# Spreading layer 0's dst values along the free axis: a DMA through DRAM in place of a 0/1 matmul

## The chip, the cores and the metric

The kernel runs on one core of one Trainium2 chip. The metric is the device time of one launch in microseconds (us). Three runs of the kernel before gave a median of 3661.84 us (3660.82 to 3661.86).

## The reference

The input is 128 graphs of 64 nodes with 768 features, all in fp32, and one 64 x 64 adjacency mask per graph. Two graph-attention layers follow each other; each is followed by a residual sum and a layernorm. The change touches layer 0 only:

```python
h = jnp.einsum('bnd,ade->bane', feat_in, W)              # 12 heads of 64
th = jnp.tanh(h)
attn_src = jnp.einsum('bane,aeo->bano', th, w_src)       # one value per node and head
attn_dst = jnp.einsum('bane,aeo->bano', th, w_dst)
attn = attn_src + jnp.swapaxes(attn_dst, 2, 3)           # score[n, m] = src[n] + dst[m]
attn = jnp.where(attn >= 0, attn, LEAKY_ALPHA * attn)
attn = jnp.where(~adj[:, None, :, :], -999.0, attn)
attn = jax.nn.softmax(attn, axis=-1)
feat_out = jnp.einsum('banm,bame->bane', attn, h) + b
# elu, then a gate: sigmoid(x @ H_w.T + H_b) mixes elu(feat_out) with x
```

Layer 1 is ordinary masked attention with 6 heads of 128 (q, k, v and an output product).

The point that matters: a score is a sum of one value of the query node n and one value of the key node m. With the query nodes on the partitions, `src[n]` is one value per partition, but `dst[m]` has to lie along the free axis and be the same on all partitions of the graph. The sums over features leave it the other way round, with node m on partition m.

## The kernel before

A *tile* is 128 tokens on the 128 partitions, which is two graphs of 64 nodes; there are 64 tiles. A *group* is two tiles (G = 2). Layer 0 works in *units*: half of the heads (6) of one tile, so there are 128 units, 4 in a group. Layer 1 works by groups.

All weights are loaded into SBUF once at the start, by DMAs issued from SyncE's queue (SP): first the first two tiles of x, then W, the broadcast vectors, H_w (transposed on TensorE), and the four weights of layer 1. The tiles of x have seven buffers, so they are loaded well ahead. Every load and store in the kernel is issued from SP.

One unit of layer 0 goes like this:

- `l0_products(u)`: the tile is transposed on TensorE (L170, first half only), and multiplied with `w_sb` (L177; 6 products of 128x384, each in two fp32 passes). VectorE (DVE) copies the result to `h` (L246), ScalarE (ACT) takes its tanh `th` (L248), GpSimd (POOL) multiplies with the src weights (L250), DVE sums over the features (L252), and POOL and DVE do the same for dst (L255, L256). Both sums are in `sd`. Then POOL builds `dg` (L261): six 64 x 64 diagonal matrices, one for each head, with dst on the diagonal. After that comes the gate's product with `hw_sb` (L177), its bias (L271) and its tanh (L272).
- `l0_probs(u)`: one matmul (L280) multiplies `same_graph`, a 0/1 matrix with a one wherever two partitions belong to the same graph, with `dg`. Its result `pd` in PSUM holds dst[m] on all partitions of the graph. DVE adds src (L282), takes the leaky part (L283); POOL and DVE apply the mask (L284, L287); `softmax` follows (L185 to L194: DVE, ACT, DVE, and POOL at the end).
- `l0_probs_transposed(u)`: TensorE transposes the probabilities (L202), and ACT and DVE copy them to `pts[0]` (L209).
- `l0_rest(u)`: the products of probabilities and `h` (L303), the elu, the gate and the residual (L308 to L324), and after a tile's second half the layernorm (L214 to L220).

The main loop goes through the units and does parts of a unit one step late, with pieces of layer 1 in between:

```python
    for u in range(NT * 2 + LAG):
        ...
            l0_products(u)
        if 0 < u <= NT * 2:
            l0_probs_transposed(u - 1)
        fill(quota // 3)
        if u < NT * 2:
            l0_probs(u)
        if 0 < u <= NT * 2:
            l0_rest(u - 1)
        fill(quota - quota // 3)
```

`fill(n)` takes pieces of layer 1 from a list until their weight reaches n: scores of one head (5; L345, L355, L358), values (4; L177 with `wv_sb`), context (2; L379, L388) and result (4; L177 with `wf_sb`, L396, then layernorm and the store at L399). The list of a group is filled at step u = 4q + 1 and lasts for four steps. The pieces of steps 0 to 5 are missing, since no group is through layer 0 yet.

The order on each engine is set by a scheduler when the program is built. It follows the source's order as a priority, but an instruction whose inputs it expects to be ready may be placed ahead of one that is earlier in the source. All waits between engines are inserted automatically, and each engine then runs its own list in order.

Of the kernel before, what the change touches and what calls it, by code (L numbers as in the profile page):

```python
# [9 lines left out]
F32 = mybir.dt.float32  # L10
U8 = mybir.dt.uint8
AF = mybir.ActivationFunctionType
ALU = mybir.AluOpType
AX = mybir.AxisListType

P = 128
# [7 lines left out]
def kernel(  # L24
# [17 lines left out]
    bf: bass.AP,  # L42
    out: bass.AP,
):
    """Two graph-attention layers, each followed by a residual and a layernorm.

    A tile is 128 tokens on the partitions: two graphs of 64 nodes. A group is G tiles, whose
    q and k share a pass over the weights. All products are in fp32.
    """
    nc = tc.nc  # L50
    NB, S, D = x.shape
    A, _, E = W.shape
# [3 lines left out]
    HALF = D // 2  # L56
    AH = A // 2
    CH = NC // 2
    G = 2
# [8 lines left out]
    const = ctx.enter_context(tc.tile_pool(name="const", bufs=1))  # L68
    xp = ctx.enter_context(tc.tile_pool(name="xp", bufs=7))
    big = ctx.enter_context(tc.tile_pool(name="big", bufs=1))  # L70
    work = ctx.enter_context(tc.tile_pool(name="work", bufs=2))
    small = ctx.enter_context(tc.tile_pool(name="small", bufs=3))
    psm = ctx.enter_context(tc.tile_pool(name="psm", bufs=4, space=bass.MemoryType.PSUM))
    psa = ctx.enter_context(tc.tile_pool(name="psa", bufs=4, space=bass.MemoryType.PSUM))

# [1 line left out]
    ident = const.tile([P, P], F32, name="ident")  # L77
    make_identity(nc, ident)
    eye = const.tile([P, S], F32, name="eye")
    nc.vector.tensor_add(eye, ident[:, :S], ident[:, S:])  # L80
    same_graph = const.tile([P, P], F32, name="same_graph")
    nc.vector.memset(same_graph, 0.0)
    for g in range(2):
        nc.vector.memset(same_graph[g * S : (g + 1) * S, g * S : (g + 1) * S], 1.0)
    neg_half = const.tile([P, 1], F32, name="neg_half")
    nc.vector.memset(neg_half, -0.5)

    xs, adjs = {}, {}
# [10 lines left out]
        load_x(t)  # L99
    load_adj(0)  # L100

# [1 line left out]
    def rows(src, name):  # L103
        n = src.shape[0]
        t = const.tile([P, n], F32, name=name)
# [15 lines left out]
    for oc in range(NC):  # L121
        hrow = xp.tile([P, D], F32, name="x")
        nc.sync.dma_start(hrow, H_w[oc * P : (oc + 1) * P, :])
        for half in range(2):
            ps = psa.tile([P, CH, P], F32, name="pa")
            for c in range(CH):
                k = half * CH + c
# [23 lines left out]
    bv_c = columns(bv, "bv_c")  # L151
    bf_bc = rows(bf, "bf_bc")

    # Transposed probabilities of AH heads, block-diagonal over the tile's two graphs: only the
    # diagonal blocks are written after this. One for each layer.
    pts = [const.tile([P, AH, P], F32, name=f"pt{i}") for i in range(2)]
    for pt in pts:
        nc.gpsimd.memset(pt, 0.0)

# [1 line left out]
    def halves(h):  # L161
        return slice(h * HALF, (h + 1) * HALF)

    def transposed(src, dst):
        """dst[:, c, :] = src[:, chunk c].T"""
        for half in range(2):
            ps = psa.tile([P, CH, P], F32, name="pa")
            for c in range(CH):
                k = half * CH + c
                nc.tensor.transpose(ps[:, c, :], src[:, k * P : (k + 1) * P], ident)  # L170
            nc.any.tensor_copy(dst[:, half * CH : (half + 1) * CH, :], ps)  # L171

    def product(lhsT, w, half):
        """One half of the columns of lhsT.T @ w in PSUM."""
        ps = psm.tile([P, HALF], F32, name="pm")
        for c in range(NC):
            nc.tensor.matmul(  # L177
                ps, lhsT[:, c, :], w[:, c, halves(half)], start=(c == 0), stop=(c == NC - 1)
            )
        return ps  # L180

    def softmax(s, n):
        """Over the last of s [P, n, S], in place."""
        mx = small.tile([P, AH], F32, name="mx")
        nc.vector.tensor_reduce(mx[:, :n], s, AX.X, ALU.max)  # L185
        nc.vector.tensor_tensor(
            s, s, mx[:, :n, None].to_broadcast([P, n, S]), ALU.subtract
        )
        nc.scalar.activation(s, s, AF.Exp)
        sm = small.tile([P, AH], F32, name="sm")  # L190
        nc.vector.tensor_reduce(sm[:, :n], s, AX.X, ALU.add)
        rs = small.tile([P, AH], F32, name="rs")
        nc.vector.reciprocal(rs[:, :n], sm[:, :n])  # L193
        nc.gpsimd.tensor_tensor(  # L194
            s, s, rs[:, :n, None].to_broadcast([P, n, S]), ALU.mult
        )

    def probs_transposed(s, pt):
        """s [P, AH, S] over (graph, query) -> [(graph, key), head, (graph, query)]."""
        ps = psa.tile([P, AH // 2, P], F32, name="pa")  # L200
        for j in range(AH // 2):
            nc.tensor.transpose(  # L202
                ps[:, j, :], s[:, 2 * j : 2 * j + 2, :].rearrange("p h m -> p (h m)"), ident
            )
        pt_v = pt.rearrange("p (j h) n -> p j h n", h=2)
        for g in range(2):
            own = slice(g * S, (g + 1) * S)
            for h2 in range(2):
                nc.any.tensor_copy(pt_v[own, :, h2, own], ps[h2 * S : (h2 + 1) * S, :, own])  # L209
# [20 lines left out]
        nc.vector.tensor_scalar(f1, a, 1.0, -L1_NEG, op0=ALU.subtract, op1=ALU.mult)  # L230
        masks[g] = (a, f0, f1)

# [1 line left out]
    xTs, units = {}, {}  # L234

    def l0_products(u):
        t, half = divmod(u, 2)
        hs = halves(half)
        if half == 0:
            xTs[t] = work.tile([P, NC, P], F32, name="xT")  # L240
            transposed(xs[t], xTs[t])
        xT = xTs[t] if half == 0 else xTs.pop(t)

        ph = product(xT, w_sb, half)
        h = work.tile([P, HALF], F32, name="h", bufs=3)
        nc.vector.tensor_copy(h, ph)  # L246
        th = work.tile([P, HALF], F32, name="th")
        nc.scalar.activation(th, ph, AF.Tanh)  # L248
        tmp = work.tile([P, HALF], F32, name="tmp", bufs=3)
        nc.gpsimd.tensor_tensor(tmp, th, ws_bc[:, hs], ALU.mult)  # L250
        sd = small.tile([P, 2, AH], F32, name="sd")
        nc.vector.tensor_reduce(  # L252
            sd[:, 0, :], tmp.rearrange("p (a e) -> p a e", a=AH), AX.X, ALU.add
        )
        nc.gpsimd.tensor_tensor(th, th, wd_bc[:, hs], ALU.mult)  # L255
        nc.vector.tensor_reduce(  # L256
            sd[:, 1, :], th.rearrange("p (a e) -> p a e", a=AH), AX.X, ALU.add
        )
        # dst on the diagonal: what same_graph spreads along the free axis
        dg = work.tile([P, AH, S], F32, name="tmp", bufs=3)  # L260
        nc.gpsimd.tensor_tensor(  # L261
            dg,
            eye[:, None, :].to_broadcast([P, AH, S]),
            sd[:, 1, :, None].to_broadcast([P, AH, S]),
            ALU.mult,
        )

        # gate = (1 + tanh(y / 2)) / 2
        pg = product(xT, hw_sb, half)
        gt = work.tile([P, HALF], F32, name="gt")  # L270
        nc.vector.tensor_tensor(gt, pg, hb_bc[:, hs], ALU.add)  # L271
        nc.scalar.activation(gt, gt, AF.Tanh, scale=0.5)  # L272
        units[u] = [h, gt, sd, dg]

    def l0_probs(u):
        g, i = divmod(u // 2, G)
        adjf, fill0, _ = masks[g]
        _, _, sd, dg = units[u]
        pd = psa.tile([P, AH, S], F32, name="pa")
        nc.tensor.matmul(pd, same_graph, dg, start=True, stop=True)  # L280
        s = work.tile([P, AH, S], F32, name="s0")
        nc.vector.tensor_tensor(s, pd, sd[:, 0, :, None].to_broadcast([P, AH, S]), ALU.add)  # L282
        nc.vector.scalar_tensor_tensor(s, s, LEAKY_ALPHA, s, op0=ALU.mult, op1=ALU.max)  # L283
        nc.gpsimd.tensor_tensor(  # L284
            s, s, adjf[:, i, None, :].to_broadcast([P, AH, S]), ALU.mult
        )
        nc.vector.tensor_tensor(  # L287
            s, s, fill0[:, i, None, :].to_broadcast([P, AH, S]), ALU.add
        )
        softmax(s, AH)  # L290
        units[u][2:] = [s]
# [4 lines left out]
    def l0_rest(u):  # L296
# [5 lines left out]
        for a in range(AH):  # L302
            nc.tensor.matmul(  # L303
                po[:, a, :], pts[0][:, a, :], h[:, a * E : (a + 1) * E], start=True, stop=True
            )
        # elu(z) + 1 = max(z, 0) + exp(min(z, 0))
        z = work.tile([P, HALF], F32, name="z")
        nc.vector.tensor_tensor(  # L308
            z.rearrange("p (a e) -> p a e", a=AH),
# [1 line left out]
            b_bc[:, None, :].to_broadcast([P, AH, E]),  # L311
            ALU.add,
        )
        e = work.tile([P, HALF], F32, name="tmp", bufs=3)
        nc.vector.tensor_scalar_min(e, z, 0.0)  # L315
        nc.scalar.activation(e, e, AF.Exp)  # L316
        nc.vector.scalar_tensor_tensor(z, z, 0.0, e, op0=ALU.max, op1=ALU.add)
        nc.vector.scalar_tensor_tensor(
            z, z, 1.0, xt[:, hs], op0=ALU.subtract, op1=ALU.subtract
        )  # L320
        # the residual's sum, doubled, as the layernorm's epsilon then is fourfold:
        # 2 * (2 * x + gate * (elu - x)) = 4 * x + (1 + tanh(y / 2)) * (elu - x)
        nc.vector.scalar_tensor_tensor(z, gt, 1.0, z, op0=ALU.add, op1=ALU.mult)  # L323
        nc.vector.scalar_tensor_tensor(  # L324
            xt[:, hs], xt[:, hs], 4.0, z, op0=ALU.mult, op1=ALU.add
# [1 line left out]
        if half == 1:  # L327
            layernorm(xt, 4.0 * EPS)

# [1 line left out]
    def layer1(g):  # L331
        x1T = big.tile([P, NC, G, P], F32, name="x1T")
        for i in range(G):
# [39 lines left out]
        def context(i):  # L373
            cTs[i] = work.tile([P, HEADS, P], F32, name="cT", bufs=1)
            for half in range(2):
                pc = psa.tile([P, CH, P], F32, name="pa")
                for j in range(CH):
# [5 lines left out]
                        start=True,  # L383
                        stop=True,
                    )
                # a row's probabilities sum to one, so v's bias goes straight to the context
                hds = slice(half * CH, (half + 1) * CH)
                nc.vector.tensor_tensor(  # L388
                    cTs[i][:, hds, :], pc, bv_c[:, hds, None].to_broadcast([P, CH, P]), ALU.add
# [25 lines left out]
        pieces += [(4, result, (G - 1, 0)), (4, result, (G - 1, 1))]  # L415
        return pieces

# [1 line left out]
    assert G == 2  # L419
    UG = 2 * G  # L420
    LAG = 2
# [62 lines left out]
```

## Time and profile before

| What | Value |
|---|---|
| median of three runs | 3661.84 us (3660.82 to 3661.86) |
| span of the profiled execution, first to last instruction | 3657.3 us |
| the runs above that span | 3.5 to 4.6 us |
| TensorE matmul (PE) busy | 3605.6 us, 99% |
| VectorE (DVE) / ScalarE (ACT) / GpSimd (POOL) busy | 47% / 22% / 23% |
| granted TensorE clock, mean | 0.997 |
| DMA of the hardware queue | 66.64 MB, 5.3% of 16 engines' span |

The profile is of one execution; of that execution it gives the span, and no time of its own beside it. The runs' time holds what lies around the span. A group of instructions shows its line, engine, operation, tiles (out<-in), shapes, count, then total busy time and the mean of one in ns, and after them the idle time of the engine just before these instructions with what ended it. PEld is TensorE's weight load, which lies beside its matmuls. Matmuls are pipelined, so the mean of one is longer than its share of TensorE; the distance from start to start is the better measure. SPq is SyncE's queue, which issues the DMAs. In the steady part a group of four units takes 112.6 us.

### The profile page before, as it was taken

Reading aid. Unit: us, or ns where it says so; the run is one execution under the profiler, and the core shown is the slowest. Engines: PE = TensorE matmul, PEld = TensorE weight load, DVE = VectorE, ACT = ScalarE, POOL = GpSimd, SP = SyncE. Lnnn points to the kernel's source line nnn. Section 1 sums busy time; section 2 is a strip of 40 time slices with the busy share of each in tenths; the row PEclk is TensorE's granted clock in tenths of the full one; section 3 lists DMA queues with packets and bytes.
Section 4 is the critical chain, followed back from the end, with each engine's and each line's share of the span. In section 5 each row is a group of like instructions: output and inputs, shape, how many; then the busy total and the mean of one; then the engine's idle time right before and its main releaser. Section 6 shows DMA issues by size and latency. Waiting matters only on the chain.

```text
span 3657.3 us, 40929 instructions
## 1 busy us (share of the span) xinstructions
PE 3605.6 (99%) x16228; PEld 2544.3 (70%) x16228; DVE 1721.5 (47%) x3821; ACT 810.4 (22%) x1925; POOL 852.3 (23%) x904
## 2 busy tenths in 40 slices
PE   6999999999999999999999999999999999999999
PEld 4776677766777666777667776677766677766776
DVE  4545444544444454444544454444445444454442
ACT  2222222222222222222222222222222222222221
POOL 2222212222222222122222222222222222222120
PEclk9999999999999999999999999999999999999999
DMA  6000000000000000000000000000000000000000
GB/s 204 1 18 18 18 10 9 18 18 18 9 10 18 18 18 10 9 18 18 18 18 9 9 18 18 18 9 10 18 18 18 9 10 18 18 18 14 5 5 18
DMA packets 44031, 69.25 MB, mean 19 GB/s; under 512 B 23104, under 2 KB 23104, under 8 KB 43840
## 3 DMA queue, kind: packets, MB, share of 16 engines
q1 hardware_dynamic: 43840, 66.64, 5.3%
q8 instruction: 128, 2.10, 0.2%
q14 instruction: 63, 0.52, 0.0%
HBM read 41.46 MB, written 25.17 MB: 18 GB/s over the span
## 4 chain that ended last, share of the span: by engine, by line
PE 88%; DVE 9%; POOL 1%; ACT 1%; SPq 0%; issue 0%; DMA 0%; POOLq 0%; ACTq 0%
PE pm L177 47%; PE pm L345 28%; PE pa L303 3%; PE pa L280 3%; PE pa L379 2%; PE pa L355 2%; PE pa L202 1%; DVE st L214 1%; POOL s L284 1%; DVE x L396 1%; PE pa L170 1%; DVE z L323 1%; DVE s L287 1%; DVE x L324 1%; DVE mx L185 1%; DVE s L283 1%
## 5 line engine op out<-in xcount | busy, mean ns | idle before, releaser
L345 PE MATMUL pm<-x1T,wq_sb 128*128 128x256 f32 x2304 | 560.3, 384 | 0.3 <-DVE x1T L171 0.3
L177 PE MATMUL pm<-w_sb,xT 128*128 128x384 f32 x1536 | 534.3, 494 | 13.9 <-DVE xT L171 13.4
L345 PE MATMUL pm<-x1T,wk_sb 128*128 128x256 f32 x2304 | 528.6, 379 | 0.0
L177 PE MATMUL pm<-wv_sb,x1T 128*128 128x384 f32 x1536 | 519.8, 488 | 0.0
L177 PE MATMUL pm<-wf_sb,cT 128*128 128x384 f32 x1536 | 517.9, 487 | 0.4 <-DVE cT L388 0.4
L177 PE MATMUL pm<-hw_sb,xT 128*128 128x384 f32 x1536 | 516.3, 486 | 0.0
L345 PEld LDWEIGHTS pm<-x1T,wk_sb 128*128 128x128 f32 x2304 | 437.8, 190 | 59.5
L345 PEld LDWEIGHTS pm<-x1T,wq_sb 128*128 128x128 f32 x2304 | 424.9, 190 | 62.6 <-DVE x1T L171 0.6
L177 PEld LDWEIGHTS pm<-hw_sb,xT 128*128 128x128 f32 x1536 | 291.8, 190 | 203.5
L177 PEld LDWEIGHTS pm<-w_sb,xT 128*128 128x128 f32 x1536 | 284.6, 190 | 199.8 <-DVE xT L171 21.1
L177 PEld LDWEIGHTS pm<-wf_sb,cT 128*128 128x128 f32 x1536 | 286.9, 190 | 187.3 <-DVE cT L388 0.7
L177 PEld LDWEIGHTS pm<-wv_sb,x1T 128*128 128x128 f32 x1536 | 284.3, 190 | 173.4
L358 DVE SCALAR_TENSOR_TENSOR s<-pa,fill 128x128 f32<-128x128 f32 x192 | 54.9, 286 | 661.7 <-PE pa L355 661.7
L250 POOL TENSOR_TENSOR tmp<-th,ws_bc 128x384 f32<-128x384 f32 x128 | 127.6, 997 | 903.7 <-ACT th L248 872.8
L194 POOL TENSOR_TENSOR s<-s,rs 128x384 f32<-128x384 f32 x192 | 177.2, 930 | 666.3 <-DVE rs L193 666.3
L284 POOL TENSOR_TENSOR s<-s,adjf 128x384 f32<-128x384 f32 x128 | 127.7, 998 | 717.1 <-DVE s L283 717.1
L209 ACT COPY pt<-pa 64x192 f32<-64x192 f32 x637 | 199.6, 313 | 428.0 <-PE pa L202 407.3
L303 PEld LDWEIGHTS pa<-h,pt 128*128 128x128 f32 x1536 | 195.4, 194 | 35.3 <-ACT pt L209 1.2
L246 DVE COPY h<-pm 128x384 f32<-128x384 f32 x128 | 71.3, 557 | 285.1 <-PE pm L177 285.1
L248 ACT ACTIVATE th<-pm 128x384 f32<-128x384 f32 x128 | 62.9, 491 | 592.6 <-DVE h L246 592.6
L303 PE MATMUL pa<-h,pt 128*128 128x64 f32 x1536 | 189.1, 273 | 0.1
L316 ACT ACTIVATE tmp<-tmp 128x384 f32<-128x384 f32 x128 | 66.9, 523 | 474.4 <-DVE tmp L315 474.4
(65 smaller groups left out, 3482.8 us busy)
## 6 DMA issues: line engine op xcount, KB each, us to landing
x<-in_x_dram SPq DMA_DIRECT2D x64, 384.0 KB, 2.9
out_dram<-x SPq DMA_DIRECT2D x64, 384.0 KB, 2.3
w_sb<-in_L_gnn_W_dram SPq DMA_DIRECT2D x6, 384.0 KB, 6.3
x<-in_L_gnn_H_w_dram SPq DMA_DIRECT2D x6, 384.0 KB, 7.2
wq_sb<-in_L_gnn_Wq_dram SPq DMA_DIRECT2D x6, 384.0 KB, 6.4
wk_sb<-in_L_gnn_Wk_dram SPq DMA_DIRECT2D x6, 384.0 KB, 7.8
wv_sb<-in_L_gnn_Wv_dram SPq DMA_DIRECT2D x6, 384.0 KB, 7.8
wf_sb<-in_L_gnn_Wf_dram SPq DMA_DIRECT2D x6, 384.0 KB, 7.8
```

Of the source, the lines that this page charges most:

```text
L177: nc.tensor.matmul(ps, lhsT[:, c, :], w[:, c, halves(half)], start=(c == 0), stop=(c == NC - 1))
L194: nc.gpsimd.tensor_tensor(s, s, rs[:, :n, None].to_broadcast([P, n, S]), ALU.mult)
L209: nc.any.tensor_copy(pt_v[own, :, h2, own], ps[h2 * S : (h2 + 1) * S, :, own])
L246: nc.vector.tensor_copy(h, ph)
L250: nc.gpsimd.tensor_tensor(tmp, th, ws_bc[:, hs], ALU.mult)
L280: nc.tensor.matmul(pd, same_graph, dg, start=True, stop=True)
L284: nc.gpsimd.tensor_tensor(s, s, adjf[:, i, None, :].to_broadcast([P, AH, S]), ALU.mult)
L303: nc.tensor.matmul(po[:, a, :], pts[0][:, a, :], h[:, a * E : (a + 1) * E], start=True, stop=True)
L316: nc.scalar.activation(e, e, AF.Exp)
L345: nc.tensor.matmul(ps, w[:, c, cols], x1T[:, c, :, :], start=(c == 0), stop=(c == NC - 1))
L355: nc.tensor.matmul(pc[own, i, :], qk[0][:, i, own], qk[1][:, i, own], start=True, stop=True)
L379: nc.tensor.matmul(pc[:, j, :], vs[i][:, hd * P : (hd + 1) * P], pts[1][:, hd, :], start=True, stop=True,)
```

## The change

`dg`, `eye`, `same_graph` and the matmul are gone. In their place each unit writes its dst sums to a small DRAM tensor `dd`, transposed while it is written (so each value is a piece of 4 bytes), and reads each graph's 6 x 64 values back to all 64 partitions of that graph, straight into `s`. This is done per graph, so there are two writes and two reads per unit, all from SP. DVE's first step then adds src to `s` in place. The buffers named `tmp`, which `dg` shared, go from three to two.

```diff
+    dram = ctx.enter_context(tc.tile_pool(name="dram", bufs=4, space=bass.MemoryType.DRAM))
...
-    eye = const.tile([P, S], F32, name="eye")
-    nc.vector.tensor_add(eye, ident[:, :S], ident[:, S:])
-    same_graph = const.tile([P, P], F32, name="same_graph")
-    nc.vector.memset(same_graph, 0.0)
-    for g in range(2):
-        nc.vector.memset(same_graph[g * S : (g + 1) * S, g * S : (g + 1) * S], 1.0)
...
     def l0_products(u):
...
-        tmp = work.tile([P, HALF], F32, name="tmp", bufs=3)
+        tmp = work.tile([P, HALF], F32, name="tmp")
...
-        dg = work.tile([P, AH, S], F32, name="tmp", bufs=3)
-        nc.gpsimd.tensor_tensor(
-            dg,
-            eye[:, None, :].to_broadcast([P, AH, S]),
-            sd[:, 1, :, None].to_broadcast([P, AH, S]),
-            ALU.mult,
-        )
+        dd = dram.tile([2, AH, S], F32, name="dd")
+        s = work.tile([P, AH, S], F32, name="s0")
+        with nc.allow_non_contiguous_dma(reason="a transpose of 6 values per node"):
+            for g in range(2):
+                nc.sync.dma_start(
+                    dd[g].rearrange("a m -> m a"), sd[g * S : (g + 1) * S, 1, :]
+                )
+                nc.sync.dma_start(
+                    s[g * S : (g + 1) * S].rearrange("p a m -> p (a m)"),
+                    dd[g : g + 1].rearrange("g a m -> g (a m)").to_broadcast([S, AH * S]),
+                )
...
-        units[u] = [h, gt, sd, dg]
+        units[u] = [h, gt, sd, s]

     def l0_probs(u):
...
-        _, _, sd, dg = units[u]
-        pd = psa.tile([P, AH, S], F32, name="pa")
-        nc.tensor.matmul(pd, same_graph, dg, start=True, stop=True)
-        s = work.tile([P, AH, S], F32, name="s0")
-        nc.vector.tensor_tensor(s, pd, sd[:, 0, :, None].to_broadcast([P, AH, S]), ALU.add)
+        _, _, sd, s = units[u]
+        nc.vector.tensor_tensor(s, s, sd[:, 0, :, None].to_broadcast([P, AH, S]), ALU.add)
```

In `l0_rest`, the third user of `tmp` loses its `bufs=3` in the same way.

More of the change, by code (lines that the diff above doesn't have):

```diff
@@ L313, in l0_rest @@
         )
-        e = work.tile([P, HALF], F32, name="tmp", bufs=3)
+        e = work.tile([P, HALF], F32, name="tmp")
         nc.vector.tensor_scalar_min(e, z, 0.0)
```

## The prediction

> **What bounds the kernel now.** I read the page's busy shares and its chain first, then the groups by line, the waits, and the timeline of one group of four units in the steady part.
>
> From the page, busy time by engine and the chain that ended last:
>
> ```profile
> PE 3605.6 (99%) x16228; PEld 2544.3 (70%) x16228; DVE 1721.5 (47%) x3821; ACT 810.4 (22%) x1925; POOL 852.3 (23%) x904
> ...
> PE 88%; DVE 9%; POOL 1%; ACT 1%; SPq 0%; issue 0%; DMA 0%; POOLq 0%; ACTq 0%
> ```
>
> TensorE is never idle for long: it is the bound, and what leaves it is gained unless a wait takes its place. From the groups by line with shapes kept apart, the matmul that goes and the POOL product that feeds it:
>
> ```profile
> L280 PE MATMUL pa<-tmp,same_graph 128*128 128x384 f32 x256 | 111.3, 517 | 8.8 <-POOL tmp L261 8.8
> L261 POOL TENSOR_TENSOR tmp<-eye,sd 128x384 f32<-128x384 f32 x128 | 106.1, 829 | 91.4 <-DVE sd L256 88.5 <-DVE mv L216 1.5 <-PE pa L202 1.5
> ```
>
> Each fp32 product is two passes, so 256 records are 128 units. A record's 517 ns is no price: passes overlap. The price is the step from start to start in the timeline. Here is the tightest of the four units of a group (start, duration, engine, line):
>
> ```profile
> 2009.62 0.55 DVE L256 TENSOR_REDUCE sd<-th 128x6 f32<-128x384 f32 x1 [0.52 <-POOL th L255]
> ...
> 2011.64 0.81 PE L280 MATMUL pa<-tmp,same_graph 128*128 128x384 f32 x2
> 2011.96 3.74 PEld L177 LDWEIGHTS pm<-wf_sb,cT 128*128 128x128 f32 x12
> 2012.29 4.03 PE L177 MATMUL pm<-wf_sb,cT 128*128 128x384 f32 x12
> 2012.49 0.56 DVE L282 TENSOR_TENSOR s<-pa,sd 128x384 f32<-128x384 f32 x1
> ...
> 2018.39 0.83 POOL L194 TENSOR_TENSOR s<-s,rs 128x384 f32<-128x384 f32 x1 [3.69 <-DVE rs L193]
> ...
> 2023.33 0.49 PE L202 MATMUL pa<-ident,s 128*128 128x128 f32 x3
> ```
>
> The row to watch is the distance from L256's end (2010.17), when the dst sums exist, to L202 (2023.33), when TensorE transposes that unit's probabilities: 13.1 us. In it lie 2.3 us up to L282 and 6.7 us of chain from L282 to the end of L194 (2019.22); 4.1 us are spare.
>
> **What goes.** L280 to the next matmul's start is 0.65 us (2011.64 to 2012.29). After the score products of L355, where 62 of the 128 stand, it is 0.75 us, of which some is the change of shape. Summed over all 128 it is 90.7 us; at 0.65 each it is 83. I take 86 us off TensorE. POOL loses 128 x 0.83 = 106 us, at 23% busy beside a full TensorE: nothing, except that the 0.83 us stood in front of L280. L282 reads s instead of PSUM; L287, which reads SBUF, takes the same 558 ns: nothing. The constants eye and same_graph (under 0.7 us together on DVE, before the first weights land): nothing. One of four "pa" buffers is asked for less often. Three to two "tmp" buffers: dg was the third user, and each of the two others is read within about 2 us of its writing (L250 to L252, L315 to L317): nothing; if their turn went wrong, it would be a wait of that size on POOL.
>
> **What comes.** Four DMAs per unit on SP's queue, 512 in all: per graph one that writes 64 x 6 values of 4 B to DRAM (W) and one that reads 1536 B back to each of 64 partitions (R, 98 KB). R waits for W's landing, L282 for both R. The trace has these neighbours (us to landing at the end):
>
> ```profile
> x<-in_x_dram SPq DMA_DIRECT2D x64, 384.0 KB, 2.9
> out_dram<-x SPq DMA_DIRECT2D x64, 384.0 KB, 2.3
> ...
> adj<-in_adj_dram SPq DMA_DIRECT2D x32, 16.0 KB, 1.7
> ...
> bq_c<-in_L_gnn_bq_dram SPq DMA_DIRECT2D x1, 3.0 KB, 7.4
> ```
>
> W: at least 1.7 (adj, 256 pieces of 64 B), at most 7.4 (bq_c, 768 pieces of 4 B, but behind the weights in the queue; the load just before it took as long). I take 2.5, the store's 2.3 and a little for the pieces, because the store is the row that writes DRAM in an empty queue. R lies between adj and x: 2.1, bounds 1.7 and 2.9. An issue holds SP for 0.34 to 0.45 us. If both W go out first, graph 1 ends last: 0.4 + 2.5, R of graph 0 ahead on SP 0.4, then 2.1: L = 5.4 us from sd to s. If SP keeps W, R, W, R, it is 2.5 + 0.4 + 2.5 + 2.1 = 7.5. The bounds are 0.4 + 1.7 + 1.7 = 3.8 and 7.4 + 0.4 + 2.9 = 10.7.
>
> The page "DMA: Bandwidth & Descriptors" of the Trainium skill speaks against this change: under "Rules for kernel authors" an access whose last dimension is strided becomes one descriptor per element, and under "Specifications" pieces below 512 B are read, modified and written. Its section "Anatomy of one DMA" gives about 2.0 us fixed per DMA, for another issuing path, mostly the receipt of the write. No row here shows pieces of 4 B written to DRAM, so nothing confirms or denies the first two; by the third alone an estimate of L is 0.4 + 2.0 + 0.4 + 2.2 = 5.0 us, and the sum below would be about 12 us better.
>
> **Where L meets slack.** Same reading (L256's end to that unit's L202) for the four units of a group, counted from the step 4q+2: 32.6, 22.0, 26.9 and 13.1 us, alike in all groups. Minus the 0.7 us that TensorE no longer spends on L280, only the last unit (step 4q+1, whose stage before L202 is short) is near: 12.4 us. It needs L + 6.7, plus contention: s now starts near 2015.6, and from 2017.6 to 2022.3 DVE also has L396, L308, L214, L315, L317, L318 and L323; I add 1.0 us, two of their steps of 0.56 (bounds 0 and 2.5). So 5.4 + 6.7 + 1.0 = 13.1 against 12.4: TensorE waits 0.7 us in each of 30 groups, 21 us. The engines' order isn't the source's order (here L202 runs ahead of both products of the next unit, which stand before it in the source), so L202 may come after those products, 8 us later; the wait then goes, but L202 no longer covers the wait for xT (0.45 us, 13.4 us in all at L177), and that costs about the same.
>
> Queued behind L282 on DVE while it waits are the evacuations of L396 and L388. Their PSUM has four buffers, and in the unit of 13.1 us the next, L396, comes at 2017.6, after the landing; in the next tightest, L388 is due 3.5 us after L282: nothing, until L passes 8. On SP the stores (L399) and loads of x come behind R's wait. The load of x is issued 2.35 us after the store and used groups later (seven buffers): nothing. SP's waits for adj and for the store end on DVE events in DVE's order, and the last such pair here (2005.38, 2007.73) is done before sd exists. R writes the s0 buffer that unit u-2 used, whose L202 is long past.
>
> **The start** is priced apart. SP there issues the weights until 50.60 us, and the first sd exists at 35.92. Nothing holds the weights back, so I expect the first W behind them, and what is issued there lands in 5 to 6 us. s is then there at 50.6 + 5.5 + 5.5 = 61.6 and the first L202 at 68.3 instead of 45.4: 23 us. TensorE can do the next tile's products meanwhile (8.2 us a unit, but gt has two buffers, so about one unit), leaving about 14; the waits for L261 there (8.8 us) end, but each of the next five units has L of 5.4 in place of about 2.1 against 1 to 5 us spare, some 8 us. Together I take +13; bounds 0 (W ahead of the weights) and 30.
>
> **Sum.** The profiled span of 3657.3 us minus 86, plus 21, plus 13 is 3605; the median of the runs, 3661.84, lies 4.5 us above the span, so 3610 us.
>
> **Rivals.**
> - *The round trip outlasts the slack* (slower). If L202's place stays and L passes 7.1 us, TensorE's wait at 30 groups, L + 7.7 - 12.4 each, exceeds the 73 us that are left after the start. At L = 8.5 it is 3.8 x 30 = 114 us, with 20 for the start: 3662 - 86 + 134 = 3710. At 10.7 it would be 180: 3776. For it: pieces of 4 B into DRAM in no row, W, R, W, R at 7.5, and a chain already fully used. Against it: stores and small loads land in 1.7 to 2.9 us, and L202 can move.
> - *All is hidden*: L near 4, W early at the start: 3662 - 88 = 3574. For it adj's 1.7; against it the order on SP.
> - *The matmul goes and the same time comes back as waits*: two effects meet near L = 7, 3655 to 3668.
> - That the change leaves the matmul in is excluded: L280 and dg are gone from the code.
>
> **How the numbers follow.** About 0.2% (7 us) is what a measurement of this kernel can tell from no change. The forecast (3580 to 3640, its own range) 0.46; all hidden 0.09; a small gain up to 3655 0.04; the meeting near zero 0.06; slower 0.35, most of it between 3670 and 3740. So faster 0.59, same 0.06, slower 0.35. The range from 3572 to 3735 leaves out some 0.03 below and 0.12 above.
>
> **What would show it.** PE busy falls by 80 to 110 us and POOL by 106. L282's idle time names a DMA from dd as releaser. W lands in 2 to 3 us, R in about 2, L is 5 to 6. PE's idle before L202, if any, is in the last unit of a group, 0 to 1 us. SP's first W is at 50 us or later. The forecast is wrong if W takes over 4 us, if SP issues W, R, W, R, or if TensorE idles in more than one unit of a group.

## The result and the profile after

The changed kernel takes 4715.7 us (median of four runs, 4705.3 to 4717.8) beside 3661.3 us before: a ratio of 1.2875, 95% interval [1.2856, 1.2893]. It is 28.8% slower. The forecast was 3610 us, with a range up to 3735.

The page of the kernel after: busy time, the granted TensorE clock in 40 slices (9 is 90% or more), the chain of work that ended last by engine, and one of the costliest groups.

```profile
PE 3829.3 (81%) x15972; PEld 2657.9 (56%) x15972; DVE 1782.2 (38%) x3816; ACT 796.0 (17%) x1926; POOL 756.1 (16%) x776
...
PEclk7889888898888888898898989888989898898999
...
PE 36%; DMA 33%; DVE 17%; POOL 8%; ACT 3%; issue 2%; SPq 1%; DVEq 0%; POOLq 0%; ACTq 0%
...
L278 DVE TENSOR_TENSOR s<-s,sd 128x384 f32<-128x384 f32 x128 | 71.5, 559 | 1450.1 <-DMA s<-dd 1450.1
```

The matmul is gone (256 records fewer), but TensorE is busy for 224 us longer and idle for 831 us more. DMA now holds a third of the chain. L278 is the old L282, the add of src: DVE stands in front of it for 11.4 us per unit (1450.1 / 127).

The issues of the two transfers follow (KB each, median us from issue to landing). W is the write of the sums to DRAM, R the read back, and L below the time from the sums to the add. The page lists R first:

```profile
s<-dd SPq DMA_DIRECT2D x256, 96.0 KB, 3.6
...
dd<-sd SPq DMA_DIRECT2D x256, 1.5 KB, 8.0
```

W takes 8.0 us where I took 2.5, R 3.6 where I took 2.1. The timeline of the tightest unit, the counterpart of the one shown before (lines are 5 lower: L251 was L256, L189 was L194, L197 was L202):

```profile
2043.94 0.55 DVE L251 TENSOR_REDUCE sd<-th 128x6 f32<-128x384 f32 x1 [0.52 <-POOL th L250]
...
2044.52 1.29 SPq L259 DMA_DIRECT2D dd<-sd  x2
...
2053.09 1.12 SPq L262 DMA_DIRECT2D s<-dd  x2
...
2057.13 0.56 DVE L278 TENSOR_TENSOR s<-s,sd 128x384 f32<-128x384 f32 x1 [10.42 <-DMA s<-dd]
...
2063.76 1.04 POOL L189 TENSOR_TENSOR s<-s,rs 128x384 f32<-128x384 f32 x1 [4.35 <-ACT x1T L166]
...
2064.85 0.90 PE L197 MATMUL pa<-ident,s 128*128 128x128 f32 x3
```

SP does issue both W before both R, as forecast; but from the end of L251 (2044.49) to L278 there are 12.6 us, not 5.4. Now the waits of the kernel after (us in total, times, longest):

```profile
DVE s L278 <- DMA s<-dd: 1450.1, 127, 21.4
ACT s L184 <- DVE s L181: 1373.7, 159, 26.0
...
PE pa L351 <- ACT kT L345: 411.7, 62, 7.9
...
PE pm L172 <- DVE cT L384: 182.5, 31, 7.1
...
PE pa L165 <- DVE z L304: 157.1, 30, 6.1
```

TensorE hardly ever waits for the delayed probabilities themselves. It waits for ACT's copy of k, for DVE's copy of the context, and for a PSUM buffer that DVE has to empty. None of the three reads the dst values that DVE waits for. A unit with score products shows how they come to be late:

```profile
2074.92 0.56 DVE L270 TENSOR_TENSOR gt<-pm,hb_bc 128x384 f32<-128x384 f32 x1
2074.95 1.29 SPq L259 DMA_DIRECT2D dd<-sd  x2
...
2088.40 0.56 DVE L278 TENSOR_TENSOR s<-s,sd 128x384 f32<-128x384 f32 x1 [12.93 <-DMA s<-dd]
...
2092.48 0.52 ACT L184 ACTIVATE s<-s 128x384 f32<-128x384 f32 x1 [11.91 <-DVE s L181]
...
2094.67 0.47 ACT L345 ACTIVATE kT<-pm,bk_c 128x256 f32<-128x256 f32 x1
...
2095.19 0.69 PE L351 MATMUL pa<-kT,qT 128*64 128x64 f32 x8 [7.17 <-ACT kT L345]
```

DVE holds at L278 until 2088.40. ACT's next instruction is that unit's exponential (L184), and it holds until DVE has gone on. Behind L184 in ACT's list stand L312 and then the copies of q and k (L345). TensorE needs k for L351 and idles 7.2 us. So a wait on one engine has passed through the list of a second to stop a third.

**Where the 1055 us of span went.** The group of four units takes 145.4 us instead of 112.6 in the steady part. Of the 32.8 us, 25.4 are longer idle time of TensorE (775.5 against 14.1 us over the 30 groups from unit 8 on). The matmul itself gives back 2.8. The remainder is 10.2 for matmuls that run slower: 976 us of the span have the clock granted at half, against 22 us before, whose row of the clock is this:

```profile
PEclk9999999999999999999999999999999999999999
```

The start takes 75 us more (DVE copies unit 8's first product at 252.5 us instead of 177.5).

### The profile page after: what moved, and what is told of

It is laid out like the page before. It is cut to its first block, busy times and chain, and to the rows that moved or that the text cites. A ratio compares the mean times of both kernels' runs of the same rounds, so it can differ in the third digit from the quotient of the medians.

```text
span 4712.3 us, 41162 instructions
## 1 busy us (share of the span) xinstructions
PE 3829.3 (81%) x15972; PEld 2657.9 (56%) x15972; DVE 1782.2 (38%) x3816; ACT 796.0 (17%) x1926; POOL 756.1 (16%) x776
## 4 chain that ended last, share of the span: by engine, by line
PE 36%; DMA 33%; DVE 17%; POOL 8%; ACT 3%; issue 2%; SPq 1%; DVEq 0%; POOLq 0%; ACTq 0%
PE pm L172 24%; DMA dd<-sd 23%; DMA s<-dd 9%; PE pm L341 9%; POOL s L280 3%; POOL th L250 3%; POOL tmp L245 3%; DVE s L279 2%; DVE s L283 2%; DVE s L278 2%; PE pa L351 2%; DVE h L241 1%; DVE sd L251 1%; DVE mx L180 1%; ACT th L243 1%
## 5 line engine op out<-in xcount | busy, mean ns | idle before, releaser
L172 PE MATMUL pm<-wf_sb,cT 128*128 128x384 f32 x1536 | 584.5, 535 | 182.5 <-DVE cT L384 182.5
L278 DVE TENSOR_TENSOR s<-s,sd 128x384 f32<-128x384 f32 x128 | 71.5, 559 | 1450.1 <-DMA s<-dd 1450.1
L341 PE MATMUL pm<-x1T,wq_sb 128*128 128x256 f32 x2304 | 613.5, 411 | 0.3 <-DVE x1T L166 0.3
L172 PE MATMUL pm<-wv_sb,x1T 128*128 128x384 f32 x1536 | 578.5, 531 | 0.0
L172 PE MATMUL pm<-w_sb,xT 128*128 128x384 f32 x1536 | 573.3, 520 | 4.8 <-DVE rstd L213 4.3
L351 PE MATMUL pa<-kT,qT 128*64 128x64 f32 x1536 | 102.0, 264 | 411.7 <-ACT kT L345 411.7
L280 POOL TENSOR_TENSOR s<-s,adjf 128x384 f32<-128x384 f32 x128 | 128.0, 1000 | 1857.8 <-DVE s L279 1857.8
L351 PEld LDWEIGHTS pa<-kT,qT 128*64 128x64 f32 x1536 | 72.4, 162 | 494.8 <-ACT kT L345 494.8
L184 ACT ACTIVATE s<-s 128x384 f32<-128x384 f32 x192 | 98.7, 523 | 1373.7 <-DVE s L181 1373.7
L165 PE MATMUL pa<-ident,x 128*128 128x128 f32 x768 | 142.3, 335 | 189.6 <-DVE z L304 157.1
L189 POOL TENSOR_TENSOR s<-s,rs 128x384 f32<-128x384 f32 x192 | 169.8, 891 | 722.7 <-DVE rs L188 575.9
L165 PEld LDWEIGHTS pa<-ident,x 128*128 128x128 f32 x768 | 110.9, 172 | 227.9 <-DVE z L304 164.2
```

The lines of the kernel that those rows point to most:

```text
L172: nc.tensor.matmul(ps, lhsT[:, c, :], w[:, c, halves(half)], start=(c == 0), stop=(c == NC - 1))
L189: nc.gpsimd.tensor_tensor(s, s, rs[:, :n, None].to_broadcast([P, n, S]), ALU.mult)
L278: nc.vector.tensor_tensor(s, s, sd[:, 0, :, None].to_broadcast([P, AH, S]), ALU.add)
L280: nc.gpsimd.tensor_tensor(s, s, adjf[:, i, None, :].to_broadcast([P, AH, S]), ALU.mult)
L341: nc.tensor.matmul(ps, w[:, c, cols], x1T[:, c, :, :], start=(c == 0), stop=(c == NC - 1))
L351: nc.tensor.matmul(pc[own, i, :], qk[0][:, i, own], qk[1][:, i, own], start=True, stop=True)
```

## The experiments

Of the experiments, e4, e5 and e6 ran several times; the others ran once each.

The theory after these readings, A: W's landing was mis-sized by 5.5 us, and what makes it cost so much is the place of the add in DVE's list, with ACT's copies behind it, and the halved clock that follows each wait. The rivals: a small write to DRAM that a read waits for costs 8 us whatever its form (B), or the transfers disturb the rest by themselves (C).

**e1: W in 64 pieces of 24 B.**

```diff
-                    dd[g].rearrange("a m -> m a"), sd[g * S : (g + 1) * S, 1, :]
+                    dd[g].rearrange("a m -> (a m)").rearrange("(m a) -> m a", a=AH),
+                    sd[g * S : (g + 1) * S, 1, :],
```

> The write W keeps its 1.5 KB per graph but puts each node's six values side by side in DRAM, so it has 64 pieces of 24 B in place of 384 of 4 B; the read back is untouched (the values come back in another order, so the scores are not the reference's). The engines' orders are those of the changed kernel. Theory A (the number of 4 B pieces written to DRAM makes W's landing 8 us instead of my 2.5): W lands in 2 to 2.8 us, sd to the add 6 to 7 us instead of 12.8; TensorE waited 5 to 7 us per unit with 12.8, so it now waits 0 to 0.7, its clock is above 0.98, and the time is 3580 to 3680 us. Theory B (any small write to DRAM that a read waits for costs 8 us here): W 7 to 8 us, the time stays at 4600 to 4720.

Measured: 3672.1 us. Its DMA issues, TensorE's two largest waits, and DVE's wait at the add:

```profile
s<-dd SPq DMA_DIRECT2D x256, 96.0 KB, 2.7
dd<-sd SPq DMA_DIRECT2D x256, 1.5 KB, 1.8
```

```profile
PE pa L197 <- POOL s L189: 44.3, 25, 22.7
PE pm L172 <- DVE rstd L213: 43.4, 30, 1.5
```

```profile
DVE s L279 <- DMA s<-dd: 532.5, 124, 13.9
```

W lands in 1.8 us, the add comes 5.3 us after the sums (median; 5.4 was the forecast's L), the changed kernel's waits of 4.3 to 7.9 us are gone, and the clock is back at 0.993. A small write is not slow as such: B falls. But 3672 us is not 3610. This kernel has the forecast's round trip and is still 10 us slower than before. A group takes 112.0 us where the sum had some 110.6; TensorE's wait of 1.4 us per group for the copies of xT, 0.45 before, is a good part of that (the row names L213, but the product starts 0.06 us after DVE's copy of xT ends). And DVE copies unit 8's first product at 207.5 us, 30 later than before, where the sum had the start cost 13.

**e2: one write per unit.** W only for g = 0, and both reads take `dd[0:1]`.

> Only graph 0's W is issued, and both reads take its row (graph 1 gets graph 0's dst values): 384 pieces of 4 B in flight per unit in place of 768. Theory A (pieces drain one after another): W lands in 4 to 5 us, sd to the add about 9, TensorE waits some 2.5 us per unit, time 3900 to 4150. Rival (W's time is fixed per transfer, or set by 24 pieces on each DMA engine): W stays at 7 to 8 us, time above 4500.

Measured: 4727.6 us, and W as slow as ever:

```profile
dd<-sd SPq DMA_DIRECT2D x128, 1.5 KB, 8.1
```

Half the pieces in flight change nothing: what makes W slow sits inside one transfer.

**e3: nobody reads the result.** R writes to a tile of its own; the add takes `h` in the place of `s`.

> All 512 DMAs stay as in the changed kernel, but their result goes to a tile that nobody reads; the add takes h in place of dst (the scores lack dst). Theory A (the loss is DVE's wait at the add, with what stands behind it on DVE and ACT): TensorE idles 25 to 60 us in all, clock above 0.98, 3575 to 3600 us. Rival C (the small DMAs disturb other transfers, SP's queue or SBUF access by themselves): above 3650.

Measured: 3664.6 us, which lies in the range of rival C (above 3650). But the trace names another cause. With nothing to wait for, the add and the chain behind it were ordered earlier on the engines, and another wait came up:

```profile
PE pa L302 <- ACT pt L204: 76.8, 37, 8.9
```

L302 is the old L303. TensorE waits there for ACT's copies of the transposed probabilities, 2.0 us per group (58.6 us from unit 8 on), and a group takes 112.6 us, as before. After 12 of the 30 waits from unit 8 on, each just under 2 us, the clock was also granted at half for 3.41 us. So the run doesn't separate C from A: it changed the order as well as the wait. It does show that the transfers alone (W 8.1 us, R 3.7) go along with a kernel within 0.1% of before, and that the matmul's removal can vanish in the order of the engines.

**e4: the add one step later.** The transfers and their 4 B pieces stay.

```diff
+            gate = l0_products(u)
...
-        if u < NT * 2:
-            l0_probs(u)
-        if 0 < u <= NT * 2:
-            l0_rest(u - 1)
+        if 0 <= u - 1 < NT * 2:
+            with tc.issue_after(gate.ins):
+                l0_probs(u - 1)
+        if 0 <= u - 2 < NT * 2:
+            l0_rest(u - 2)
```

`gate` is the gate's sum of unit u, and `issue_after` puts the add behind it on DVE. `l0_probs_transposed` and layer 1 move by one step too; `h`, `gt`, `s0` and `sd` get one buffer more, x has six.

> The DMAs and the 4 B pieces stay, and all values are right. The probabilities of a unit are made one step later: the add of unit u-1 is queued on DVE behind the gate's sum of unit u, 22 to 33 us after that unit's sums, and everything after it moves by one step (h, gt, s0 and sd have one buffer more each, x one less). Theory A (the round trip of 12.8 us costs only because the add stands at the head of DVE's in-order queue, and ACT's evacuations behind it): DVE's wait at the add disappears except at the start, TensorE is 98 to 99% busy at full clock, 3575 to 3625 us, which is below both kernels. Rival C (the transfers cost by themselves): above 3700.

Measured: 3626.6 us, a ratio of 0.9904 [0.9887, 0.9920] to before, about 1% faster than the kernel before, and 1.6 us above the range. The page's busy line, then the DMA wait at the add (L279 here):

```profile
PE 3541.4 (98%) x15972; PEld 2500.7 (69%) x15972; DVE 1735.0 (48%) x3783; ACT 822.9 (23%) x1959; POOL 727.9 (20%) x776
```

```profile
DVE s L279 <- DMA s<-dd: 18.9, 3, 9.5
```

W still takes 8.1 us. DVE waits 18.9 us in all instead of 1450, and a group takes 110.8 us. That is the same round trip, free once something else stands in front of its consumer: C falls, and A holds.

**e5: the matmul for the first six units.** e4, but units 0 to 5 spread dst with `same_graph`. The tile z has one buffer, and the constants lie in a buffer of x.

> As the version that makes the probabilities one step later, but the first six units (before layer 1 has any work) still spread dst with the 0/1 matmul; from unit 6 on it is the DMA. All values are right. In e4 unit 0's add came at 67.7 us, because its writes were issued behind the weights. Theory A (e4's loss at the start is the round trip behind the weights' transfers): unit 8's first product is done 15 to 25 us earlier than e4's 171.3 us, the steady group stays at 110.8 us, 3600 to 3613 us. Rival (the start is bound by the later step itself, or by the loading of weights): within 5 us of e4's 3626.6.

Measured: 3614.2 us, 0.9873 [0.9856, 0.9889] to before, 1 us above the range and the fastest of all. Unit 8's first product is copied at 157.4 us instead of e4's 171.3, 14 us earlier where I had 15 to 25. The start does pay for the round trip behind the weights.

**e6: e4's order with the matmul.** All units use `same_graph`, no DMA for dst; z has one buffer here too.

> The control of e4: the same order with the probabilities one step later and the same number of x buffers, but dst is spread by the 0/1 matmul in all units, no DMA at all (z has one buffer, to make room). All values are right. Theory A (in e4 the matmul's removal is worth 1.8 us per group and the later step by itself nothing): a group takes 112.4 to 112.9 us and the time is 3650 to 3675 us. Rival (the later step is itself the gain): below 3640 us.

Measured: 3663.0 us, 1.0005 [0.9996, 1.0014]; a group takes 112.9 us. Its busy line has the 256 records of the matmul back:

```profile
PE 3606.0 (98%) x16228; PEld 2536.6 (69%) x16228; DVE 1720.4 (47%) x3851; ACT 801.1 (22%) x1895; POOL 854.5 (23%) x904
```

The later step by itself gives nothing in the whole. In equal order the DMA in place of the matmul is worth 112.93 - 110.78 = 2.15 us per group.

**e7 and e11: needless products in a wait.** The changed kernel with 20 (e7) or 36 (e11) products more, ahead of the scores of heads 0 and 4:

```diff
+            for _ in range(20 if hd in (0, 4) else 0):
+                nc.tensor.matmul(pc, ident, wq_sb[:, 0, :P], start=True, stop=True)
```

> The changed kernel with 20 needless 128x128 products (into a buffer that is then overwritten) ahead of the score products of heads 0 and 4, where TensorE waited 6.6 us in two units of four; all values are right. They cost about 0.23 us each, 4.7 us in the unit, 9.4 us per group. Theory A (after such a wait the granted clock is halved for 6.8 us, which costs 3.4 us beside the wait): the half-clock time per group falls from 29.5 us to 13 to 18, and the time falls by 100 to 220 us, to 4490 to 4615, although work is added. Rival (the low clock follows from the whole idle share or from nothing that the waits do): same or longer, 4700 to 5000.

> As e7, with 36 needless products in place of 20: 8.2 us of them where TensorE waited 6.6 us. In e7 a wait of 3.5 us stayed, and the half-clock time fell to 24.8 us per group only. Theory A (a wait beyond some 3 us is followed by 6.8 us at half clock): the wait at the scores is below 1.5 us in the two units, half-clock time is 13 to 17 us per group, a group takes 141 to 146 us, 4570 to 4740 us in all. Rival (the clock follows the mean load, which this raises little): half-clock time stays over 22 us per group, above 4850 us.

e7 took 4811.6 us, which is in the rival's range and not in A's. Some 3.5 us of each wait stayed, and with them most of the half clock, some 25 us per group:

```profile
PE pa L353 <- ACT kT L345: 217.7, 62, 4.7
```

So e7 alone does not tell the two apart. e11 covers the wait (the same row, then its page's busy line):

```profile
PE pa L353 <- ACT kT L345: 14.9, 23, 1.7
```

```profile
PE 4208.6 (89%) x20580; PEld 3098.4 (66%) x20580; DVE 1780.7 (38%) x3816; ACT 795.1 (17%) x1926; POOL 758.0 (16%) x776
```

It takes 4713.5 us, with 16.3 us more work on TensorE per group than the changed kernel in the same time, and its half-clock time falls from 29.5 to 15.3 us per group, as expected: two of the four waits of a group are gone, and so are two of the four stretches. That is against the rival, which had over 22 us per group.

**e8, e9, e10: what makes W slow.** e8 writes three heads (192 pieces of 4 B), and the reads take these twice. e9 gives each of the 384 pieces its own 64 B, e10 lays them in node order, 8 B apart (its buffers are `[2, S, AH, 2]` and the write goes to `dd[g, :, :, 0]`). e9's edit:

```diff
+    dds = [dram.tile([2, AH, S, 16], F32, name=f"dd{i}", bufs=1) for i in range(4)]
...
-                    dd[g].rearrange("a m -> m a"), sd[g * S : (g + 1) * S, 1, :]
+                    dd[g, :, :, 0].rearrange("a m -> m a"), sd[g * S : (g + 1) * S, 1, :]
```

> W writes the dst values of three heads alone, 192 pieces of 4 B per graph in place of 384; the read back comes in two DMAs per graph that both read these three rows (heads 3 to 5 get the values of heads 0 to 2). Theory A2 (W's landing grows with the pieces of one DMA, 0.3 us for each of the 24 on a DMA engine; two DMAs beside each other don't add, as e2 showed): W lands in 4 to 5 us, sd to the add 9 to 10.5 us with the two extra reads, time 4000 to 4400. Rival (8 us is what any write of 4 B pieces costs): W 7.5 to 8.5, time 4700 to 4850.

> W keeps its 384 pieces of 4 B per graph, but each piece goes to its own 64 B of DRAM (four buffers of 48 KB, zeroed at the start); the read back takes the first 1536 B of the same buffer, so the scores don't hold the right dst values. Theory A3 (writes of 4 B that fall into the same 64 B of DRAM wait for one another: 16 of them there in the changed kernel, which is the same for 192 or 384 pieces and for one or two transfers, as e8 and e2 had it): W lands in 2 to 3.5 us, sd to the add 6 to 7.5 us, time 3650 to 3800. Rival A2 (the count of pieces, not linear): W stays at 7 to 8.5, time 4600 to 4750.

> 384 pieces of 4 B per graph again, in the order of the nodes, 8 B apart: the 24 values that one DMA engine takes (four nodes) lie together in 192 B, and a 64 B stretch holds 8 pieces of one engine, not 16 of four engines. The read back takes the first 1536 B of the same buffer (half of it zeros, so not the right dst values). Theory A3 with the sharing between engines as its cause: W 2 to 3.5 us, 3650 to 3800. A3 with the mere number of pieces in 64 B: about half of 8 us, 4 to 5 us, 3900 to 4200. Rival A2: 7 to 8.5 us, 4600 to 4750.

Measured: 4650.5, 3687.0 and 3997.3 us. W in e8, e9 and e10, in this order:

```profile
dd<-sd SPq DMA_DIRECT2D x256, 0.8 KB, 7.1
```

```profile
dd<-sd SPq DMA_DIRECT2D x256, 1.5 KB, 2.1
```

```profile
dd<-sd SPq DMA_DIRECT2D x256, 1.5 KB, 4.5
```

Half the pieces cost almost the same (7.1, between the two expectations), so the count is not the main cause: A2 falls. As many pieces as in the changed kernel, each in 64 B of its own, land in 2.1 us. With 8 pieces to a 64 B stretch it is 4.5, with 16 it is 8.0. The steps are alike, (4.5 - 2.1) / 7 = 0.34 us and (8.0 - 4.5) / 8 = 0.44 us for each further piece in the same 64 B. e10 lays the pieces of four neighbouring nodes side by side. If each DMA engine takes four neighbouring nodes, which no trace here shows, a stretch is written by one engine and still costs time, which speaks for the number of pieces and against the sharing between engines. That the stretch is just 64 B, and not some other length, was not varied. Nor is this a rule for longer pieces: e1's 24 B pieces also share 64 B, some 2.7 to a stretch, and land in 1.8 us.

## Why the prediction was wrong, by its steps

**The matmul's worth** was 86 us. L280's own steps are 2.79 us per group, 89 us in all; in equal order (e5 against e6) 2.15 us per group are left, 69 us. The other 0.6 comes back before L303 and the context product, which stood behind L280; presumably it gave their inputs time to come. It was a small cover that I priced at nothing.

**W, the term that failed first.** I took 2.5 us "because the store is the row that writes DRAM in an empty queue", with an upper bound of 7.4 from bq_c. It is 8.0, above the bound. The store's pieces are 3072 B long and never share 64 B, and bq_c is a read. Neither row has the property that costs here, and I chose by the kind of transfer. R was 3.6 beside W's 4 B pieces and 2.7 in e1. L was 12.7, beyond its upper end of 10.7.

The page "DMA: Bandwidth & Descriptors" of the Trainium skill, under "Rules for kernel authors", warns of a strided last dimension because it makes one descriptor per element, and under "Specifications" of a read-modify-write below 512 B. The warning was right for this change. The runs put its cost elsewhere: 384 single elements land in 2.1 us when they don't share 64 B, and 24 B pieces, also far below 512 B, in 1.8.

**What is behind L282** was the deeper error. My slack table asked only when TensorE needs that unit's probabilities, and found one unit of four near. I named L396 and L388 on DVE as queued behind, "nothing, until L passes 8", and never followed the queue to ACT, where L189's exponential (L184 after) stands ahead of the copies of q and k (L349, L345 after). From unit 8 on, TensorE waits 6.6 and 6.7 us at the scores in two units, 6.1 at the result product and 6.3 at the transposes of the other two: all four units, 25.7 us per group. The two waits at the scores come through ACT. The other two come from DVE's own list, where the context's copy (L384, the old L388) and the sum that empties a PSUM buffer (L304, the old L308) stand behind the add. My rival "the round trip outlasts the slack" had the right first cause and charged it at one unit: 3776 us at its far end. Two of the three signs that I had given for a wrong forecast came: W over 4 us, and TensorE idle in more than one unit of a group.

**The clock** was not in the sum at all. In the changed kernel each of the 120 TensorE waits over 3 us from unit 8 on has a stretch at half clock, typically 6.83 us, that begins during it; in the steady part of e1 and e4 there is none of either. That the one brings the other is what e11 supports. The page "TensorE: Matmul & The Clock Gate" of the Trainium skill, under "HAM oscillation", gives idle gaps of more than about 3.4 us as the limit. The 120 waits here, all over 4.3 us, agree, but the limit is not sharp: 15 of 16 waits of 2 to 3 us in e7 and 12 of 30 of nearly 2 us in e3 had a stretch at half clock too.

**The start** was +13. e1, with my L, lost 30 us up to unit 8, and the changed kernel 75. That W is issued behind the weights was right (51.8 us); that TensorE would work ahead meanwhile was too hopeful, and each of the next units paid the longer chain.

**Even with W right the forecast of faster would have failed**: e1 and e9 have L near 5.3 and 5.9 and take 3672 and 3687 us. The right idea, that the matmul's time can be had if the round trip is covered, holds only with the cover built (e4, e5).

## What to carry to other kernels

When a wait is put in front of an instruction, follow the lists of all engines, not only of the one that waits: what does the next engine run after the delayed result, and who needs the thing behind that? A round trip through DRAM is affordable when its consumer is queued a step later than its producer; give the consumer a place behind other work rather than trusting that the round trip is short. Where a transfer's price is taken from another row, match what the pieces do to memory (length and neighbours), not only the direction and the queue.

## What the runs showed of the hardware that I had not expected

- Writes of 4 B to DRAM that share 64 B, from issue to landing: 8.0 us with 16 in a stretch, 4.5 with 8, 2.1 with one, for the same 384 pieces; half the pieces at 16 to a stretch still take 7.1 us.
- In the changed kernel each TensorE wait over 4.3 us in the steady part brought some 6.8 us at half clock; in e3, 12 of 30 waits of nearly 2 us brought 3.41 us. Filling two of four such waits per group with needless products (e11) halved the half-clock time, and the kernel took no longer (4713.5 against 4715.7 us).
